# Layer 1's attention scores: a pair's half products issued in two steps, and later blocks' moves queued behind the fourth pair's copies

## The chip, the cores and the metric

The kernel runs on one core of one Trainium2 chip. The metric is the device time of one execution in microseconds (us); before the change three runs had a median of 2338.59 us. In the profile PE is TensorE (matrix products; PEld its weight loads), DVE is VectorE, ACT is ScalarE, POOL is GpSimd and SP is SyncE, which here only issues DMAs. "L753" is line 753 of the kernel before; the change moves later lines by a few (L753 becomes L756, L835 becomes L839, L852 becomes L856).

## The reference

The reference computes two layers in float32. Layer 0 is a convolution-style attention with 8 heads on 8 batch elements of 1024 positions and 256 channels. Layer 1 is what the change touches, followed by a mixture of 8 experts:

```python
def _L1_attn_ref(x, W):
    xa = jnp.einsum('bnd,ed->bne', x, W)
    scores = jnp.einsum('bne,bme->bnm', xa, x)
    attn = jax.nn.softmax(scores, axis=-1)
    return jnp.einsum('bnm,bmd->bnd', attn, x)

x = _L0_conv_ref(x, ...)
t = _to_tokens(x)
t = t + _L1_attn_ref(_ln_t(t), L1_attn_W)
t = t + _L1_ffn_ref(_ln_t(t), router_w, w1, b1, w2, b2)
```

So for each batch element there is a 1024 x 1024 matrix of scores, a softmax over its rows, and a product of the result with the 1024 x 256 normalised tokens.

## The kernel before

The eight batch elements are worked on one after the other. An element goes through layer 0 (`layer0`), then layer 1's attention (`attend`), then a norm and the router. Elements 0 to 6 are sent to the experts sorted by expert, all together near the end (`experts`); element 7 goes through all experts densely (`dense`), while the sorted results of the others are gathered and added beside it.

In `attend` the 1024 rows of scores are eight blocks of 128 rows. The scores are made by Strassen's scheme in the form with seven products: the sums and differences of the operands are `s1_` to `s4_` and `t1_` to `t4_`, and two blocks, k and k+4, form a `Pair`. A pair needs seven half products of 128 x 512 results (L753). They go to three places in PSUM: `x` and `v` are the two halves of one tile of 1024 columns (`both`, the profile's `ps`), and `z` is a tile of its own (`ps1z`). The products into `x` accumulate, and between them the intermediate sum is copied out by ACT: the first copy (L741) after a11 b11, the second (L745) after s2 t2 is added, the third (L748) after s3 t3 is added. Each of the next products into `x` therefore waits for the copy before it. DVE then adds `v` or `z` to a copy and takes the row minimum in the same instruction (`add`, L763). `rest` adds the last two products, ends the row maxima (L763 and L791), and ACT takes the exponentials (L786, L795, L803).

A block of exponentials must be transposed before the mixing, which is the product with the tokens. `turn` does it without TensorE: DVE transposes squares of 32 x 32 (L824), and sixteen moves (L835) bring the squares to their places, eight as ACT copies and eight as DMAs that SP issues, in turns. `turn_now` does it on TensorE for the first and the last block (L842, `pa`). `mix` is the mixing: eight products of 128 x 256 into `py` (L852), then DVE adds the result to the tokens (L861). The mixings run in the order of the blocks 0, 4, 1, 5, 2, 6, 3, 7; the profile's numbers for `py` in this text are block numbers. The code's own names `first`, `second`, ... `eighth` follow that same order.

The order of the instructions on each engine is made by the program before it runs: the statements are recorded, and a list scheduler with its own costs sets them in order under their data dependencies. `tc.issue_after(a)` asks that what follows stand behind `a`; `tc.declare_no_dep` takes a dependency away. Each engine then runs its list strictly in order. Elements 1 to 6 have the same order as one another. Elements 0 to 6 also have parts of the next element's layer 0 between the mixings (`pv`, L408). In element 7 DVE also adds the gathered expert results (`o`, L1400), placed by the table `PLACES` behind named steps of the attention.

Of the kernel before, what the change touches and what calls it, by code (L numbers as in the profile page):

```python
# [12 lines left out]
AF = mybir.ActivationFunctionType  # L13
# [6 lines left out]
def kernel(  # L20
# [23 lines left out]
    nc = tc.nc  # L44
    P = 128
# [43 lines left out]
    def big(name):  # L89

        return ps_big.tile([P, 1024], F32, tag="big", name=name)

    def acc(name):

        return ps_acc.tile([P, 512], F32, tag="acc", name=name)
# [234 lines left out]
    evicted = {}  # L330
# [342 lines left out]
    def attend(b, t1, fill, tick=nothing):  # L673
# [13 lines left out]
        HALF = S // 2  # L687
# [3 lines left out]
        t1_, t2_, t3_, t4_ = (mixes[:, i, :] for i in range(4))  # L691
# [5 lines left out]
        s1_, s2_, s4_ = (mixes[:, 4 + i, :] for i in range(3))  # L697
# [27 lines left out]
        class Pair:  # L725

            def __init__(self, k):
                self.k = k
                both = big(f"ps1_{b}_{k}")
                self.x, v = both[:, :HALF], both[:, HALF:]  # L730
                self.z = acc(f"ps1z_{b}_{k}")
                self.ex = [homes[EX[2 * k + h]] for h in range(2)]
                self.low = [
                    small.tile([P, 1], F32, tag=f"nlow{h}", name=f"nlow_{b}_{k}_{h}")
                    for h in range(2)
                ]
                left, right = (self.ex[0][:, ts(n, HALF)] for n in range(2))
                far = self.ex[1][:, ts(1, HALF)]
                at = ts(k, P)
                self.product(self.x, a11, b11, True)  # L740
                self.first = nc.scalar.copy(left, self.x)  # L741
                second = self.product(v, a12, b21, True)
                tc.declare_no_dep(second.ins, self.first.ins, reason="the other bank")
                self.product(self.x, s2_, t2_, False)
                self.second = nc.scalar.copy(right, self.x)  # L745
                self.product(self.z, s1_, t1_, True)
                self.product(self.x, s3_, t3_, False)
                nc.scalar.copy(far, self.x)  # L748
                self.add(left, v, 3.0e38, self.low[0])
                self.add(far, self.z, 3.0e38, self.low[1])  # L750

            def product(self, to, stationary, moving, start):
                return nc.tensor.matmul(  # L753
                    to,
                    stationary[:, ts(self.k, P)],
                    moving,  # L756
                    start=start,
                    stop=True,
                    skip_group_check=not start,
                )  # L760
# [10 lines left out]
                    accum_out=to,  # L771
                )

            def rest(self):
                k = self.k
                self.product(self.z, s4_, b22, False)
                self.product(self.x, a22, t4_, False)
                nmax, ssum = [], []
                for h in range(2):
                    nmax.append(small.tile([P, 1], F32, tag="nmax", name=f"nmax_{b}_{2 * k + h}"))  # L780
                    ssum.append(small.tile([P, 2], F32, tag="ssum", name=f"ssum_{b}_{2 * k + h}"))
                ex0, ex1 = self.ex

                def even():
                    tick(("max", 2 * k), self.add(ex0[:, HALF:], self.z, self.low[0], nmax[0]))
                    nc.scalar.activation(  # L786
                        ex0, ex0, AF.Exp, bias=nmax[0], scale=-1.0, accum_out=ssum[0][:, 0:1]
                    )

                def odd():  # L790
                    last = nc.vector.tensor_scalar(  # L791
                        scrap, self.x, -1.0, self.low[1], ALU.mult, ALU.min, accum_out=nmax[1]
                    )
                    tick(("max", 2 * k + 1), last)
                    nc.scalar.activation(  # L795
                        ex1[:, :HALF],
                        self.x,
                        AF.Exp,
                        bias=nmax[1],
                        scale=1.0,  # L800
                        accum_out=ssum[1][:, 0:1],
                    )
                    nc.scalar.activation(  # L803
                        ex1[:, HALF:],
                        ex1[:, HALF:],
                        AF.Exp,
                        bias=nmax[1],
                        scale=-1.0,
                        accum_out=ssum[1][:, 1:2],
                    )  # L810

                for half in (odd, even) if k == 1 else (even, odd):
                    half()
                return [(2 * k, ex0, ssum[0][:, 0:1], None), (2 * k + 1, ex1, *self.halves(ssum[1]))]
# [4 lines left out]
        def turn(i, ex, behind=None):  # L819


            at_sq, at_aT = SQ_AT[i]
            sq = homes[at_sq]
            nc.vector.transpose(sq, ex)  # L824
            if at_aT is None:
                aT = two.tile([P, S], F32, tag="tr", name=f"aT_{b}_{i}")
            else:
                aT = homes[at_aT]
            to = aT.rearrange("p (m a q) -> p a m q", a=NQ, q=SQ)
            since = sq.rearrange("p (m k q) -> p k m q", k=NQ, q=SQ)  # L830
            for a in range(NQ):
                for k in range(NQ):
                    move = nc.sync.dma_start if (a + k) % 2 else nc.scalar.copy
                    with tc.issue_after(behind[a * 2 // NQ].ins) if behind else nullcontext():
                        move(to[ts(k, SQ), a], since[ts(a, SQ), k])  # L835
            return [aT[:, ts(m, P)] for m in range(NT)]
# [10 lines left out]
        def mix(at, aT, ssum, more):  # L847
            i = BLOCKS[at]
            ahead = fill("last products") if at == NT - 1 else None
            py = acc(f"py_{b}_{i}")  # L850
            for m in range(NT):
                evicted["mixed"] = nc.tensor.matmul(  # L852
                    py[:, :D], aT[m], n1[:, m, :], start=(m == 0), stop=(m == NT - 1)
                )
            rs = small.tile([P, 1], F32, tag="rs1", name=f"rs1_{b}_{i}")
            if more is not None:  # L856
                nc.vector.tensor_add(rs, ssum, more)
                ssum = rs
            nc.vector.reciprocal(rs, ssum)
            with tc.issue_after(ahead.ins) if ahead else nullcontext():  # L860
                mixed = nc.vector.scalar_tensor_tensor(  # L861
                    t2[:, i, :], py[:, :D], rs, t1[:, i, :], ALU.mult, ALU.add
                )
            tick(("mixed", at), mixed)
# [3 lines left out]
        def turned(at, ex, ssum, more, behind=None):  # L868
            return at, turn(at, ex, behind), ssum, more

        pairs = [Pair(0), Pair(1)]
        first, second = pairs[0].rest()
        second = turned(*second)
        third, fourth = pairs[1].rest()
        now = turn_now(0, first[1])
        pairs.append(Pair(2))
        third = turned(*third, (pairs[2].first, pairs[2].second))
        fourth = turned(*fourth, (pairs[2].second, pairs[2].second))
        mix(0, now, *first[2:])
        mix(*second)  # L880
        fifth, sixth = pairs[2].rest()
        fifth = turned(*fifth)
        mix(*third)
        pairs.append(Pair(3))
        sixth = turned(*sixth, (pairs[3].second, pairs[3].second))
        mix(*fourth)
        seventh, eighth = pairs[3].rest()
        seventh = turned(*seventh)
# [3 lines left out]
        now = turn_now(7, eighth[1])  # L892
# [428 lines left out]
    class Results:  # L1321
# [96 lines left out]
        def tick(self, place, behind=None):  # L1418
            added, sent, stored = self.PLACES.get(place, (0, 0, 0))
            if place == ("max", 0):  # L1420
                self.scored = behind
            if added:
                with tc.issue_after(behind.ins):
                    for _ in range(added):
                        self.add()
            for _ in range(sent):
                self.gather(behind)
            for _ in range(stored):
                if self.whole:
                    b, total, n = self.whole.pop(0)  # L1430
                    store(b, total, n)
# [135 lines left out]
    for b in range(B):  # L1567
# [18 lines left out]
        def fill(place):  # L1586

            nonlocal norm
            others.tick(place)
            if place == "last products":  # L1590
                norm = Norm(t1, one.tile([P, NT, D], F32, tag="xa", name=f"n2_{b}"), 1e-5, f"f{b}")
                return norm.blocks(0, NT - 1)
# [46 lines left out]
```

## Time and profile before

| what | value |
|---|---|
| three runs | 2336.98, 2345.87, 2338.59 us |
| median | 2338.59 us |
| the profiled execution's own time | 2327.18 us |
| its span | 2325.2 us |
| mean granted TensorE clock | 0.993 |
| PE busy | 2259.1 us, 97% of the span |
| DVE, ACT, POOL busy | 67%, 50%, 18% |
| `attend`, px to the last py, elements 1 to 6 | 67.03 to 67.53 us each |
| the same of element 0 | 74.76 us |
| the same of element 7 | 73.15 us |

Times are microseconds from the span's start. A row of the timeline gives the start, the length of a merged run of instructions, the engine, the line, the operation and the tiles, the count, and in brackets the idle time of the engine just before it with what ended that idle time. A half product is recorded as two passes of TensorE ("x2"). PE rows overlap a little, since a product's end is recorded after the next has begun.

### The profile page before, as it was taken

To read this page: it belongs to the slowest core of one execution; us is meant where nothing else is said; L and a number is where in the kernel's file an instruction comes from. 1 tells how busy PE (TensorE), PEld (TensorE's weight loads), DVE (VectorE), ACT (ScalarE), POOL (GpSimd) and SP (SyncE) were. 2 spreads that over 40 slices of the span, in tenths; PEclk is the share of its full clock that TensorE was granted. 3 is DMA by queue.
4 is the path that set the end of the run, shared out by engine and by line. 5 is a ranking of instruction groups with operands and counts; after the bars stand their busy time and mean duration, and the time that the engine had idled before them with its cause. 6 is when DMAs were issued, how large, how long until landed. Compare 5 with 4: busy or idle time off the path is not lost.

```text
span 2325.2 us, 37960 instructions
## 1 busy us (share of the span) xinstructions
PE 2259.1 (97%) x13059; PEld 1211.7 (52%) x13059; DVE 1561.8 (67%) x4029; ACT 1167.0 (50%) x2139; POOL 411.2 (18%) x392
## 2 busy tenths in 40 slices
PE   9999999999999999999999999999999899999798
PEld 3344634563356335643554355435553278886565
DVE  5775678567865786578757775677668756435765
ACT  3664466356635663656464656465546532224311
POOL 0000012000200030003000200021002124544663
PEclk9999999999999999999999999999999999999899
DMA  8995201020102010201020101100120237765664
GB/s 293 385 386 156 69 12 45 4 61 8 49 1 55 12 53 1 46 19 51 6 40 25 44 13 24 41 21 17 19 45 19 71 90 196 194 190 156 189 201 134
DMA packets 278759, 200.10 MB, mean 86 GB/s; under 512 B 189576, under 2 KB 232232, under 8 KB 276776
## 3 DMA queue, kind: packets, MB, share of 16 engines
q1 hardware_dynamic: 252472, 139.14, 21.3%
q0 software_dynamic: 25008, 58.01, 7.8%
q8 instruction: 104, 1.70, 0.3%
q10 hardware_dynamic: 1088, 0.52, 0.1%
q14 instruction: 87, 0.71, 0.1%
HBM read 108.88 MB, written 110.90 MB: 95 GB/s over the span
## 4 chain that ended last, share of the span: by engine, by line
PE 80%; ACT 6%; DVE 5%; DMA 4%; issue 3%; SPq 1%; POOL 0%; DVEq 0%; ACTq 0%; POOLq 0%
PE po L569 19%; PE psc L492 18%; PE pqk L371 7%; PE py L852 6%; PE pr L666 5%; PE pv L408 4%; PE ps L753 3%; PE ph L1256 3%; PE pe L1282 3%; PE pdy L1529 2%; PE pdh L1505 2%; PE px L703 2%; PE pqk L349 2%; DMA y<-yb 1%; ACT aT L835 1%
## 5 line engine op out<-in xcount | busy, mean ns | idle before, releaser
L533 ACT ACTIVATE ex<-psc,nmax 128x1024 f32<-128x1024 f32 x512 | 570.5, 1115 | 309.9 <-DVE scrap L516 225.9
L569 PE MATMUL po<-ex,vs 64*64 64x512 f32 x4096 | 569.6, 593 | 10.7 <-SPq L579 9.8
L492 PE MATMUL psc<-qk,qk 64*64 64x512 f32 x4096 | 573.0, 593 | 3.6 <-ACT ex L533 3.5
L516 DVE TENSOR_SCALAR_CACHE_REDUCE scrap<-psc,nmax 128x512 f32<-128x512 f32 x512 | 384.4, 751 | 166.6 <-PE psc L492 138.7
L507 DVE TENSOR_REDUCE nmax<-psc 128x1 f32<-128x512 f32 x512 | 350.3, 684 | 9.3 <-PE psc L492 9.3
L492 PEld LDWEIGHTS psc<-qk,qk 64*64 64x64 f32 x4096 | 178.7, 132 | 281.1 <-ACT ex L533 131.5
L569 PEld LDWEIGHTS po<-ex,vs 64*64 64x64 f32 x4096 | 173.1, 132 | 287.8 <-issue 84.2
L1070 POOL DMA_INDIRECT rows<-n,d_at x112 | 109.0, 973 | 663.6 <-DVE nmax L507 663.3
L997 POOL TENSOR_TENSOR t<-t,n 128x2048 f32<-128x2048 f32 x8 | 36.3, 4536 | 876.8 <-DVE n L263 876.8
L371 PE MATMUL pqk<-xT,wqkv 128*128 128x512 f32 x384 | 171.2, 599 | 0.0
L336 ACT ACTIVATE qk<-pqk,b_qks 128x512 f32<-128x512 f32 x124 | 85.6, 690 | 86.6 <-PE pqk L371 77.5
L371 PEld LDWEIGHTS pqk<-xT,wqkv 128*128 128x128 f32 x384 | 71.0, 190 | 99.9 <-issue 76.5
L1378 POOL DMA_INDIRECT yk<-y,yat x112 | 111.4, 995 | 60.4 <-issue 25.6
L408 PE MATMUL pv<-wqkv,xT 128*128 128x512 f32 x256 | 120.3, 599 | 1.6 <-DVE v L416 1.0
L852 PE MATMUL py<-n,spare 128*128 128x256 f32 x512 | 118.0, 386 | 3.9 <-DMA out_dram<-oT 3.2
L852 PEld LDWEIGHTS py<-n,spare 128*128 128x128 f32 x512 | 98.3, 193 | 29.0 <-issue 16.4
L666 PE MATMUL pr<-wo,res 128*128 128x256 f32 x512 | 111.9, 379 | 0.0
L835 ACT COPY spare<-home 32x256 f32<-32x256 f32 x256 | 103.0, 402 | 10.1 <-DVE home L824 6.7
L666 PEld LDWEIGHTS pr<-wo,res 128*128 128x128 f32 x512 | 97.2, 190 | 17.0 <-ACT res L588 3.2
L1266 ACT ACTIVATE hb<-ph,wb 128x256 f32<-128x256 f32 x96 | 40.4, 471 | 125.4 <-issue 84.0
L533 ACT ACTIVATION_READ_ACCUMULATOR ex<-psc,nmax 128x1 f32 x512 | 99.1, 194 | 0.0
L1256 PE MATMUL ph<-xb,wb 128*128 128x256 f32 x384 | 91.8, 381 | 5.7 <-DMA wb<-wpack,w_at 4.1
(256 smaller groups left out, 2889.6 us busy)
## 6 DMA issues: line engine op xcount, KB each, us to landing
rows<-wb SPq DMA_DIRECT2D x7, 8192.0 KB
xr<-rows SPq DMA_DIRECT2D x252, 64.0 KB
y<-yb POOLq DMA_DIRECT2D x63, 256.0 KB, 2.6
xs<-in_x_dram SPq DMA_DIRECT2D x64, 128.0 KB
spare<-home SPq DMA_DIRECT2D x256, 32.0 KB
out_dram<-oT SPq DMA_DIRECT2D x60, 128.0 KB
xT<-in_x_dram SPq DMA_DIRECT2D x7, 1024.0 KB
sums<-t SPq DMA_DIRECT2D x7, 1024.0 KB
```

The source lines that it names most:

```text
L371: mm = nc.tensor.matmul(pq[:, ts(n, 512)], wqkv[:, cc, t, ts(g, P)], xT[:, cc, ts(n, 512)], start=(cc == 0), stop=(cc == NCC - 1),)
L408: nc.tensor.matmul(pv, self.xT[:, cc, ts(i, P)], wqkv[:, cc, 2, :], start=(cc == 0), stop=(cc == NCC - 1),)
L492: mm = nc.tensor.matmul(pss[at, h][ts(c, DK), ts(n, 512)], k[r, j * P + c * DK : j * P + (c + 1) * DK], q[r, ts(n, 512)], start=True, stop ...
L507: firsts[at, h] = nc.vector.tensor_reduce(nmax, pss[at, h][:, ts(0, 512)], AX.X, ALU.max, negate=True)
L516: seconds[h] = nc.vector.tensor_scalar(scrap, pss[at, h][:, ts(1, 512)], -1.0, nmaxes[at, h], ALU.mult, ALU.min, accum_out=nmax,)
L533: nc.scalar.activation(ex, pss.pop((at, h)), AF.Exp, bias=nmaxes.pop((at, h)), scale=1.0, accum_out=sums[at][:, h : h + 1],)
L569: mm = nc.tensor.matmul(po[n][ts(h, DK), :], vss[at][keys, h, :], exps[at, h][keys, ts(n, 512)], start=(j == 0 and turn == 0), stop=(j == ...
L666: nc.tensor.matmul(pr[:, :C], res[:, g, ts(i, P)], wo[:, g, :], start=(g == 0), stop=(g == NPAIR - 1))
L835: move(to[ts(k, SQ), a], since[ts(a, SQ), k])
L852: evicted["mixed"] = nc.tensor.matmul(py[:, :D], aT[m], n1[:, m, :], start=(m == 0), stop=(m == NT - 1))
L1256: last = nc.tensor.matmul(ph[:, ts(fc, BR)], wb[:, dc * FF + fc * P : dc * FF + (fc + 1) * P], xb[:, dc, :], start=(dc == 0), stop=(dc == ...
L1378: ins = nc.gpsimd.indirect_dma_start(out=self.slot(at)[:, k, :], out_offset=None, in_=self.group.y[:, :], in_offset=bass.IndirectOffsetOnAxis(
```

## The change

`Pair` no longer issues its first five products in one go. Its constructor issues three of them (a11 b11, a12 b21, s1 t1), the first copy, and DVE's `add(left, v)`. A new step `middle` issues s2 t2, the second copy, s3 t3, the third copy and `add(far, z)`. For pair 2 `middle` stands behind the first mixing. For the pairs before and after it is called where the text shows. The moves of the fifth and sixth block now stand behind the fourth pair's second and third copies. `rest` takes an argument that sets the first block's exponential behind the second pair's third copy. The first mixing is emitted before the turns of the third and fourth block.

```diff
-                left, right = (self.ex[0][:, ts(n, HALF)] for n in range(2))
-                far = self.ex[1][:, ts(1, HALF)]
-                at = ts(k, P)
+                self.left = self.ex[0][:, :HALF]
                 self.product(self.x, a11, b11, True)
-                self.first = nc.scalar.copy(left, self.x)
+                self.first = nc.scalar.copy(self.left, self.x)
                 second = self.product(v, a12, b21, True)
                 tc.declare_no_dep(second.ins, self.first.ins, reason="the other bank")
-                self.product(self.x, s2_, t2_, False)
-                self.second = nc.scalar.copy(right, self.x)
                 self.product(self.z, s1_, t1_, True)
+                self.add(self.left, v, 3.0e38, self.low[0])
+
+            def middle(self, behind=None):
+                far = self.ex[1][:, HALF:]
+                with tc.issue_after(behind.ins) if behind else nullcontext():
+                    self.product(self.x, s2_, t2_, False)
+                self.second = nc.scalar.copy(self.ex[0][:, HALF:], self.x)
                 self.product(self.x, s3_, t3_, False)
-                nc.scalar.copy(far, self.x)
-                self.add(left, v, 3.0e38, self.low[0])
+                self.third = nc.scalar.copy(far, self.x)
                 self.add(far, self.z, 3.0e38, self.low[1])
+                return self
...
-            def rest(self):
+            def rest(self, behind=None):
...
-                    nc.scalar.activation(
-                        ex0, ex0, AF.Exp, bias=nmax[0], scale=-1.0, accum_out=ssum[0][:, 0:1]
-                    )
+                    with tc.issue_after(behind.ins) if behind else nullcontext():
+                        nc.scalar.activation(
+                            ex0, ex0, AF.Exp, bias=nmax[0], scale=-1.0, accum_out=ssum[0][:, 0:1]
+                        )
...
-        pairs = [Pair(0), Pair(1)]
-        first, second = pairs[0].rest()
+        pairs = [Pair(0).middle(), Pair(1).middle()]
+        first, second = pairs[0].rest(pairs[1].third)
         second = turned(*second)
         third, fourth = pairs[1].rest()
         now = turn_now(0, first[1])
         pairs.append(Pair(2))
+        mix(0, now, *first[2:])
+        pairs[2].middle(evicted["mixed"])
         third = turned(*third, (pairs[2].first, pairs[2].second))
         fourth = turned(*fourth, (pairs[2].second, pairs[2].second))
-        mix(0, now, *first[2:])
         mix(*second)
         fifth, sixth = pairs[2].rest()
-        fifth = turned(*fifth)
+        pairs.append(Pair(3))
         mix(*third)
-        pairs.append(Pair(3))
-        sixth = turned(*sixth, (pairs[3].second, pairs[3].second))
+        pairs[3].middle()
+        fifth = turned(*fifth, (pairs[3].second, pairs[3].second))
+        sixth = turned(*sixth, (pairs[3].third, pairs[3].third))
         mix(*fourth)
```

`evicted["mixed"]` is the last product of the latest mixing, and `turned(..., behind)` sets both the ACT half and the SP half of a block's moves behind the two instructions given.

## The prediction

> **What bounds the kernel now.** I read the page's engine rows and its chain first, then a table of the eight stretches of `attend`, then the timelines of PE and ACT inside three of them.
>
> ```profile
> span 2325.2 us, 37960 instructions
> PE 2259.1 (97%) x13059; PEld 1211.7 (52%) x13059; DVE 1561.8 (67%) x4029; ACT 1167.0 (50%) x2139; POOL 411.2 (18%) x392
> PE 80%; ACT 6%; DVE 5%; DMA 4%; issue 3%; SPq 1%; POOL 0%; DVEq 0%; ACTq 0%; POOLq 0%
> ```
>
> PE is the bound nearly everywhere, and the change adds and removes no product. It can only move PE's idle time, of which the whole span has 66 us (2325.2 less 2259.1). The stretches from the first px product to the last mixing (columns: length, then PE, PEld, DVE, ACT and POOL busy, and the granted clock), for elements 1, 0 and 7:
>
> ```profile
> 437.38:504.43 67.05, 64.97 (x226) 40.71 (x225) 36.02 (x85) 40.69 (x89) 0.00 (x0) 1.00 0.24 40
> 189.51:264.27 74.76, 68.93 (x226) 42.26 (x225) 35.99 (x85) 40.62 (x89) 0.00 (x0) 0.95 0.47 104
> 2113.22:2186.37 73.15, 65.39 (x216) 40.41 (x216) 53.22 (x121) 40.68 (x89) 46.69 (x48) 0.95 0.70 188
> ```
>
> PE is idle for 2.08 us in element 1 (2 to 6 are alike), 5.8 in element 0 and 7.8 in element 7. The PE timeline shows where; element 1 first, then element 0:
>
> ```profile
> 464.91 1.12 PE L753 MATMUL ps<-mixes 128*128 128x512 f32 x2 [0.47 <-ACT home L741]
> 467.18 1.12 PE L753 MATMUL ps<-mixes,xa 128*128 128x512 f32 x2 [0.28 <-ACT home L745]
> 481.69 1.12 PE L753 MATMUL ps<-mixes,xa 128*128 128x512 f32 x2 [1.33 <-ACT home L745]
> ...
> 226.39 1.12 PE L753 MATMUL ps<-mixes 128*128 128x512 f32 x2 [2.09 <-ACT home L741]
> 229.50 2.08 PE L753 MATMUL ps<-mixes,xa 128*128 128x512 f32 x2 [1.98 <-ACT home L745]
> 231.36 5.65 PE L852 MATMUL py<-n,aT 128*128 128x256 f32 x16
> ```
>
> Each wait is a product into `x` waiting for ACT's copy of what `x` held. A wait costs 0.26 us more than its bracket: products start 0.86 us apart but are recorded 1.02 long, which hides 0.16, and the product after a wait takes 1.12 instead of 1.02. So element 1 loses 2.08 + 3 x 0.26 = 2.9 us. In element 0 a mixing then takes 5.65 us where the others take 3.62, and a product 2.08 where others after a wait take 1.12. The table by 3.4 us shows why:
>
> ```profile
> 225.23:228.64 3.41, 1.12 (x2) 0.30 (x2) 0.69 (x3) 3.34 (x8) 0.00 (x0) 1.00 0.32 49
> 228.64:232.05 3.41, 2.55 (x4) 1.43 (x5) 0.32 (x2) 1.25 (x4) 0.00 (x0) 0.50 0.06 10
> 232.05:235.47 3.42, 3.42 (x9) 2.70 (x9) 0.70 (x2) 0.14 (x1) 0.00 (x0) 0.50 0.02 5
> ```
>
> After a slice with PE busy for 1.12 us the clock was halved for two slices. Price: 5.65 - 3.62 + 2.08 - 1.12 = 3.0 us. Last, ACT in element 1, on which the moves and the copies queue:
>
> ```profile
> 477.71 3.31 ACT L835 COPY home<-home 32x256 f32<-32x256 f32 x8
> 481.05 0.59 ACT L745 COPY home<-ps 128x512 f32<-128x512 f32 x1
> 481.66 1.65 ACT L835 COPY spare<-home 32x256 f32<-32x256 f32 x4
> 483.33 0.59 ACT L748 COPY home<-ps 128x512 f32<-128x512 f32 x1
> 483.94 1.64 ACT L835 COPY spare<-home 32x256 f32<-32x256 f32 x4
> 487.96 1.15 ACT L786 ACTIVATE home<-home,nmax 128x1024 f32<-128x1024 f32 x1 [2.37 <-DVE nmax L763]
> ```
>
> **The change part by part.** The order of instructions that the changed program holds, set against the old one, is the same outside `attend` on every engine, and the same on SP but for one place in element 7: a load of sums, which waits for a DVE add, now stands ahead of twelve moves. It holds them up by some 2 us (a wait of 1.4 and its issue), which the mixings of blocks 1 and 5, 5 us or more behind their last moves, cover; uncovered it would cost those 2 us. I took the durations of the rows above and walked the new order through one middle element, in the old trace's times.
>
> *First two waits (pair 2).* Old: 0.47 + 0.28 + 2 x 0.26 = 1.27 us. New: s2 t2 stands behind all eight mixing products and one `pv` product, so PE has a free slot at 461.69 (first mixing) + 8 x 0.43 + 0.86 = 466.0. But DVE's `add(left, v)` is now ahead of it in the program, it reads the other half of the tile that s2 t2 writes, and the product waits for it (the program's waits name DVE there; before it was ACT's copy). DVE ends a transposition at 465.67, or 0.15 later because the first pairs' adds are reordered, and the add takes 0.69: 466.45. Idle 0.45, and 0.10 for the restart. Then s3 t3 has its slot at 466.55 + 0.96 + 0.86 = 468.3, but the second copy now has four moves (4 x 0.415) and the fourth pair's first copy (0.59) before it on ACT: 465.85 + 1.66 + 2 x 0.59 = 468.7. Idle 0.45, restart 0.10. Sum 1.1 us: a gain of 0.2 that a late DVE add takes back, so I put it at nil (bounds -0.3 and +0.5 us).
>
> *Third wait (pair 3).* Old 1.33 + 0.26 = 1.59: the second copy stood behind eight moves (the row at 477.71). New: the fifth block's ACT moves stand behind that copy, and s2 t2 behind mixing 1. Its result is there 1.02 us after its start, the copy takes 0.59, so s3 t3 can start at 1.66 and has a slot at 0.86: idle 0.8, restart 0.1, or 0.9. Gain 0.65.
>
> *What ACT pushes back.* s2 t2 now starts at 475.03 + 0.86 + 3.45 = 479.35, so its copy ends at 481.0. Behind it ACT has sixteen moves (6.64) and the third copy (0.59), and only then the seventh block's exponential: 488.2 at the earliest, against 487.96, and 488.6 if ACT waits for the third product. The 2.37 us that ACT had idle before that row was the cover, and ACT spends it idle after 477.7 instead. From this exponential hang a DVE transposition, eight moves on SP at 0.65 us each, and mixing 3. In the trace its last move is issued at 495.09 and, by the semaphore records, lands at 497.05; mixing 3 starts at 497.3 without a wait. With PE 0.65 earlier (496.7) and the moves 0.25 to 0.65 later (497.5), PE waits 0.8 us, and a restart behind a DMA costs up to 0.26. This is a new wait of about 1.05.
>
> Sum for a middle element: 0 - 0.65 + 1.05 = +0.4 us; the bounds are -0.65 (no new wait) and +1.0 (one more ACT move and one SP issue in that chain). Times six: **+2.4 us** (-3.9 to +6).
>
> *Element 0.* Old: 5.8 idle + 6 x 0.26 = 7.3 us. New, walked the same way: 0.5 and 0.6 for pair 2; 0.9 for a22 t4 behind the third copy; 1.7 for pair 3's s3 t3, whose copy stands behind seven moves (2.9 us) that its product outruns by 1.2; 1.3 for the last block's transposes, whose exponential waits in ACT's queue; five restarts at 0.1. Together 5.5, so -1.8 (bounds -2.5, -1.0). The two waits of 2 us are no longer in one slice, so the halved clock should go: -3.0, or 0 if a slice falls badly around the 1.7.
>
> The Trainium skill, in "TensorE: Matmul & The Clock Gate" (section "Why this matters for your kernels"), asks for no PE gap over about 3 us, one idle window returning the clock to half. No gap here was over 2.1 us and the clock halved all the same, so the measurement decides; by the page's rule alone nothing would be owed to the clock in element 0, and the sum would be 3.0 higher.
>
> *Element 7.* Here DVE also adds gathered results, eight to fourteen `o` adds of 0.4 us at a step. In the new order pair 3's `add(left, v)` stands behind some thirteen of them, a store's transposition (1.2) and two maxima, and reaches 2153.7; s2 t2 now waits for that add, where in the trace it started at 2150.59 without a wait. That is 3.1 us of new idle; pair 2's two waits grow by 1.3, and one for the third copy adds 0.9. The old waits of 0.84 and 1.18 go with their 0.5, and so does most of the 1.09 at block 4's mixing. Sum +5.3 - 3.4 = **+1.9** (bounds +0.5, +4). One 3.1 us gap may halve the clock (0 to +3.4, half of 6.8); later waits hide most of it; I take +0.5.
>
> Total: 2.4 - 1.8 - 3.0 + 1.9 + 0.5 = 0.0 us. On the profiled execution's own 2327.18 that is 2327.2; that execution lies 11.4 below the median of the three runs, so on their scale the forecast is 2338.6.
>
> **The rivals.**
>
> *Faster: ACT's queue does not hold the seventh exponential.* If it starts as soon as its maximum is known, mixing 3 does not wait: 6 x -0.65 - 4.8 + 1.9 = -6.8, or 2332 us. For it: ACT is only 61% busy in element 1. Against: the sixteen moves now begin 3.3 us later.
>
> *Slower: ACT's moves late at every mixing.* If each middle element pays +1.0, element 0 keeps its half clock and element 7's gap brings one (+3.4): 6 - 1.8 + 1.9 + 3.4 = +9.5, or 2348 us. The place is ACT between the fourth pair's second copy and the seventh exponential; it decides once that stretch is over 0.65 us longer than the row's start at 487.96 allows. To pass 0.5% (11.7 us) the middle elements would need +1.4 each.
>
> *The change doesn't do what it says.* SP's half of the moves keeps its place, and the freed third product only trades one wait for another: every part near nil but the clock, -3.0 or 0, 2336 to 2339 us. This is hard to tell from the forecast.
>
> **How the numbers follow.** Forecast 0.70 (with the third rival inside it), faster rival 0.12, slower rival 0.18. The range runs from the faster rival's 2332 to the slower one's 2348, which also holds a scatter of medians, the three runs lying 9 us apart. About 0.5% is what a measurement of this kernel can tell from no change; all cases but the far ends lie inside. Slower by more than that 0.08 (the slower rival's tail), faster 0.04 (it would take -2.0 in every element, more than two thirds of the 2.9 that is lost there), the rest 0.88.
>
> **What would show it.** In elements 1 to 6: the first wait named as DVE `nlow`, the third at about 0.6 to 0.8, a new wait at block 3's mixing on `spare` moves, the stretch 67.0 to 68 long. In element 0: no halved clock, about 70 us. In element 7: one idle of 3 us at `ps<-mixes`. I am wrong if a middle element's length moves by over 1 us, or if element 0 keeps its waits of 2 us.

## The result, and the profile after

| | median | lowest to highest | runs |
|---|---|---|---|
| before | 2340.25 us | 2336.98 to 2346.86 | 15 |
| after | 2337.94 us | 2334.14 to 2342.53 | 15 |

The ratio of after to before is 0.9985, 95% interval 0.9976 to 0.9994: 3.5 us less, between 1.4 and 5.6. The forecast of no change, 0.0 us, lies outside that interval; the measured time lies inside the forecast's range. That 2337.94 is so close to the 2338.6 of the forecast is luck: with fifteen runs the kernel before has a median of 2340.25, where three had 2338.59. The profiled execution of the changed kernel took 2334.83 us. The top of its page:

```profile
span 2332.8 us, 37999 instructions
PE 2261.0 (97%) x13059; PEld 1211.5 (52%) x13059; DVE 1558.5 (67%) x4029; ACT 1167.8 (50%) x2139; POOL 411.6 (18%) x392
```

This one execution is longer than the profiled one of before (2325.2), although the median is shorter: single executions say little here, and the comparison has to be made by stretches. The profile of before (2327.18 us) also lies below all fifteen runs of before in this table. Up to the first px product of element 7 that makes no difference: it starts at 2109.22 us here, and at 2108.60 and 2110.35 in two later profiles of the same kernel. From there to the end this execution took 223.57 us and the later ones 214.43 and 212.75, so the rows of element 7 shown here are those of an unusually long execution. The stretches of `attend` for elements 1, 0 and 7 (length, then PE, PEld, DVE, ACT and POOL busy, and the clock):

```profile
432.60:499.97 67.37, 65.37 (x226) 40.53 (x225) 35.74 (x85) 40.54 (x89) 0.00 (x0) 1.00 0.24 40
189.80:259.31 69.51, 65.85 (x226) 40.36 (x225) 35.68 (x85) 40.52 (x89) 0.00 (x0) 1.00 0.51 113
2109.22:2187.95 78.73, 67.82 (x216) 41.40 (x216) 51.26 (x118) 40.84 (x89) 47.34 (x48) 0.93 0.62 167
```

Element 1 is 0.3 us longer than before, element 0 is 5.25 shorter with the clock at 1.00 instead of 0.95, element 7 is 5.6 longer. PE's timeline in element 1:

```profile
461.79 1.13 PE L756 MATMUL ps<-mixes 128*128 128x512 f32 x2 [0.22 <-DVE nlow L766]
464.11 1.13 PE L756 MATMUL ps<-mixes,xa 128*128 128x512 f32 x2 [0.33 <-ACT home L749]
476.31 1.13 PE L756 MATMUL ps<-mixes,xa 128*128 128x512 f32 x2 [0.73 <-ACT home L749]
492.82 3.48 PE L856 MATMUL py<-n,spare 128*128 128x256 f32 x15 [0.72 <-DVE t L865]
```

All four waits stand where the prediction put them. The first is now named as DVE's add (`nlow`), the third has fallen from 1.33 to 0.73, and the fourth is new, at block 3's mixing. (The DVE `t` that is named there ends at 492.62, but it is not what is waited for: in an experiment below the same mixing starts before that DVE instruction does. By the semaphore records the last of block 3's moves lands at 492.58, 0.24 us ahead of the mixing.) ACT in the same element:

```profile
475.67 0.59 ACT L749 COPY home<-ps 128x512 f32<-128x512 f32 x1 [2.67 <-PE ps L756]
...
477.84 0.59 ACT L751 COPY home<-ps 128x512 f32<-128x512 f32 x1
...
480.13 3.31 ACT L839 COPY spare<-home 32x256 f32<-32x256 f32 x8
483.47 1.15 ACT L790 ACTIVATE home<-home,nmax 128x1024 f32<-128x1024 f32 x1
```

The 2.67 us that ACT waits idle before the second copy stand in place of the 2.37 that it was idle ahead of the seventh exponential before. That exponential now starts straight behind the sixteenth move, with no bracket: ACT's queue holds it. Element 0, PE's timeline and the 3.4 us slice that holds its longest wait:

```profile
223.89 1.13 PE L756 MATMUL ps<-mixes,xa 128*128 128x512 f32 x2 [0.58 <-ACT home L751]
227.45 1.12 PE L756 MATMUL ps<-mixes,xa 128*128 128x512 f32 x2 [1.57 <-ACT home L749]
228.41 3.62 PE L856 MATMUL py<-n,aT 128*128 128x256 f32 x16
```

```profile
225.24:228.66 3.42, 1.85 (x6) 0.71 (x5) 1.43 (x4) 3.31 (x8) 0.00 (x0) 1.00 0.30 48
```

PE is busy for 1.85 us in that slice instead of 1.12, and the mixing behind it takes 3.62 us where it took 5.65: the clock is not halved. Element 7:

```profile
2138.53 1.12 PE L756 MATMUL ps<-mixes 128*128 128x512 f32 x2 [1.07 <-DVE nlow L766]
2149.80 1.64 PE L756 MATMUL ps<-mixes 128*128 128x512 f32 x2 [2.32 <-issue]
2152.07 6.17 PE L856 MATMUL py<-n,spare 128*128 128x256 f32 x16 [0.63 <-DMA spare<-home]
...
2193.56 3.60 PE L281 MATMUL pt_n<-ident,n 128*128 128x128 f32 x14 [5.61 <-DVE n L263]
```

The wait of s2 t2 for DVE's add is there (2.32; in a later profile of the same kernel it is named DVE `nlow`), and in this execution the clock was halved behind it: the mixing at 2152.07 takes 6.17 us.

### The profile page after: what moved, and what is told of

It reads as the page before. It is cut to its first block, busy times and chain, and to the rows that moved or that the text cites. A ratio compares the mean times of both kernels' runs of the same rounds, so it can differ in the third digit from the quotient of the medians.

```text
span 2332.8 us, 37999 instructions
## 1 busy us (share of the span) xinstructions
PE 2261.0 (97%) x13059; PEld 1211.5 (52%) x13059; DVE 1558.5 (67%) x4029; ACT 1167.8 (50%) x2139; POOL 411.6 (18%) x392
## 4 chain that ended last, share of the span: by engine, by line
PE 78%; DVE 5%; ACT 5%; issue 5%; DMA 3%; POOL 3%; SPq 1%; another core or an unknown queue 0%; DVEq 0%; ACTq 0%; POOLq 0%
PE po L569 18%; PE psc L492 18%; PE py L856 7%; PE pqk L371 7%; PE pr L666 5%; PE ps L756 4%; PE pv L408 4%; PE ph L1262 3%; PE pe L1288 3%; PE px L703 2%; POOL yk L1384 2%; PE pqk L349 2%; PE ps1z L756 2%; DMA y<-yb 1%; ACT aT L839 1%
## 5 line engine op out<-in xcount | busy, mean ns | idle before, releaser
L516 DVE TENSOR_SCALAR_CACHE_REDUCE scrap<-psc,nmax 128x512 f32<-128x512 f32 x512 | 384.2, 750 | 165.9 <-PE psc L492 137.3
L1384 POOL DMA_INDIRECT yk<-y,yat x112 | 111.7, 997 | 73.4 <-issue 29.2
```

The source lines that it names most:

```text
L516: seconds[h] = nc.vector.tensor_scalar(scrap, pss[at, h][:, ts(1, 512)], -1.0, nmaxes[at, h], ALU.mult, ALU.min, accum_out=nmax,)
L1384: ins = nc.gpsimd.indirect_dma_start(out=self.slot(at)[:, k, :], out_offset=None, in_=self.group.y[:, :], in_offset=bass.IndirectOffsetOnAxis(
```

## The experiments

Twelve kernels ran in three series of four, most of them eleven times and two of them five times. Each was compared with runs of the kernel before in the same series; "saved" and "lost" below are the ratio's distance from 1 times 2328, with its 95% interval. In these three series the kernel before had medians of 2327.91, 2327.49 and 2328.29, some 12 us less than in the series of the result.

### First series: the parts by themselves

The kernel before again, unchanged:

> The kernel before, unchanged, timed against itself and profiled once more. Theory A (the terms of the forecast were right, and the profiled execution of before was typical): ratio 1.000; element 7's attention again near 73 us and from its first px product to the end of the span near 212 us. Theory B (the profiled execution of before had a lucky element 7, and most executions lose some 10 us more there): ratio 1.000, but element 7's attention 75 to 79 us, or from its first px product to the end 218 to 224 us; elements 0 and 1 at 74.8 and 67.05 us as before.

Measured: ratio 1.0002 (0.9992 to 1.0012). Its profile repeats the stretches of before: element 0 74.71, element 1 67.08, element 7 73.28, the halved clock at 228.6. From px of element 7 to the end it took 213.73 us, against 211.94 in the profiled execution of before. So in this series the first profile is a typical one. For the series of the result, which was some 12 us slower, there is no profile of the kernel before.

The next three kernels hold both forms of `attend` and take the new one where a condition on the element holds:

```diff
     def attend(b, t1, fill, tick=nothing):
...
+        if b == 0:          # e0_only; mid_only: 0 < b < B - 1; e7_only: b == B - 1
+            ...             # Pair, rest, turn, mix and the order of the change
         ...                 # the same of before
```

> The new order in element 0 alone, the old one in elements 1 to 7. Theories A and B: element 0's attention near 69.5 us instead of 74.8, no halved clock in it, the time lower by 4.8 to 5.3 us (ratio 0.998). A third theory (the halved clock of element 0 falls only in some executions of before): lower by 2 to 3 us only, ratio 0.999.

Measured: ratio 0.9991 (0.9982 to 1.0), 2.1 us saved. Element 0 took 69.43, no halved clock stands in it, and px of element 1 comes 242.71 us after px of element 0, against 247.83: 5.1 us in the trace. That is more than the runs allow (0.0 to 4.2); where the rest went was not found.

> The new order in elements 1 to 6 alone. Theories A and B: each of them 67.3 to 67.6 us instead of 67.05, the time up by 2 to 2.5 us (ratio 1.001). A fourth theory (the middle elements gain in most executions): down by 2 us or more.

Measured: ratio 1.0010 (1.0001 to 1.0019), 2.3 us lost. Elements 1 to 5 took 67.31, 67.27, 67.56, 67.53 and 67.30, each 0.23 to 0.29 more than in the kernel before of this series; from px of element 1 to px of element 6 it is 1201.88 against 1200.68. The theory that the middle elements gain is out.

> The new order in element 7 alone. Theory A (the forecast's term): up by 2.4 us, or as the profile after has it by 5 or more, ratio 1.001 to 1.002. Theory B: nil or down by up to 2 us, ratio 0.999 to 1.000, since the new 3 us wait only takes the place of waits for late transfers that most executions have.

Measured: ratio 1.0009 (1.0 to 1.0018), 2.1 us lost. Element 7's attention took 77.63, which is 4.35 more, but from its px to the end it is 215.44 against 213.73, only 1.7 more. In this pair of profiles more than half of the loss is given back behind the attention.

The results also list every run's mean granted clock. The 33 runs of before average 0.9918, the 11 runs with only element 0 new 0.9929. That is 2.6 us of full clock in 2328, close to the 3.4 that one halved stretch of 6.83 us takes. In the profiles the halved clock stands in element 0 in all four kernels that have its old form unchanged (from 226.7 or 228.6 us on), and in none of the nine with the new one. So it is there in most executions, not in some.

### Second series: the whole, pairs of parts, and the term of ACT's queue

> The changed kernel itself again, in one series with kernels that hold parts of it. Theory A (the parts add up: element 0 -2.1, elements 1 to 6 +2.3, element 7 +2.1, each measured against before in the first series): +2.3 us against before, element 0 at 69.5, a middle element at 67.3 to 67.6, element 7 at 77 to 79. Theory S (the whole gains 3.5 us, and the parts do not add up, because what element 7 loses is given back when the elements before it are new as well): -3.5 us here too. Theory M (both are within what a series can shift, since the length of the first layer's expert stretch and of the tail differ by several us from one execution to the next whatever the order): between -3 and +2, with the stretches of element 0, of the middle ones and of element 7 as in the parts.

Measured: ratio 1.0 (0.9991 to 1.0009). Element 0 69.42, elements 1 to 5 67.27 to 67.52, element 7 76.62.

> The new order in elements 0 to 6, the old one in element 7. Theory A: +0.2 us against before (-2.1 + 2.3), and 2.1 less than the whole. Theory S: slower than the whole, since the new element 7 belongs to the gain; -1 or more. Theory M: 2 us less than the whole, element 7 at 73 to 74.

Measured: ratio 0.9990 (0.9981 to 0.9999), 2.3 us saved. Element 7 took 73.36. The two kernels differ in element 7 alone, and their rows show how the loss there is given back. DVE's last `o` add before the last norm, and PE's first transposition behind that norm, in the kernel with the old element 7:

```profile
2183.93 0.53 DVE L1579 SCALAR_TENSOR_TENSOR o<-yk,gate,o 128x256 f32<-128x256 f32 x1 [1.69 <-DMA yk<-y,yat]
```

```profile
2187.31 3.48 PE L281 MATMUL pt_n<-ident,n 128*128 128x128 f32 x14 [5.27 <-DVE n L263]
```

and the same in the whole change:

```profile
2185.35 0.44 DVE L1406 SCALAR_TENSOR_TENSOR o<-yk,gate,o 128x256 f32<-128x256 f32 x1
```

```profile
2188.84 3.48 PE L281 MATMUL pt_n<-ident,n 128*128 128x128 f32 x14 [3.62 <-DVE n L263]
```

With the old element 7 DVE waits 1.69 us for a gathered result of the experts before it can normalise; with the new one the result has landed by then. The attention ends 3.3 us later, the transposition starts 1.6 later.

> The new order in elements 0 and 7, the old one between. Theory A: 0.0 us against before (-2.1 + 2.1), and 2.3 less than the whole. Theory S, if the middle elements carry the gain: about +0, that is 3.5 more than the whole. Middle elements at 67.05, element 0 at 69.5 without a halved clock, element 7 at 77 to 78.

Measured: ratio 1.0002 (0.9992 to 1.0012). Elements 1 to 5 67.04 to 67.32, element 6 67.82, element 0 69.43, element 7 74.79. The three kernels of this series lie within each other's intervals, so they do not by themselves decide between the theories; the stretches do.

The fifth block's moves, in the kernel with the old element 7:

```diff
-        fifth = turned(*fifth, (pairs[3].second, pairs[3].second))
+        fifth = turned(*fifth, (pairs[3].first if b else pairs[3].second, pairs[3].second))
```

> As the new order in elements 0 to 6 with the old one in element 7, but in elements 1 to 6 the first half of the fifth block's ACT moves stands ahead of the second copy of pair 3, the second half ahead of its third copy; nothing else in any queue moves. By the forecast's term of what ACT pushes back (+1.05 a middle element: twelve moves in place of sixteen stand between the second copy and the seventh exponential, so that it starts 1.66 us earlier) the wait at block 3's mixing, 0.72 in the changed kernel, goes to 0 to 0.1, the third wait stays at 0.7, and a middle element falls by 0.7 to some 66.8: 4.3 us less than the kernel with the new order in elements 0 to 6, about -4 against before. The rival (the exponential is not held by ACT's queue but by its maximum, or block 3's moves by SP): the wait stays at 0.7 and the middle elements at 67.4, no difference. A third way: the four moves hold up the second copy, the third wait grows by as much as the other shrinks, and the length stays.

Measured: ratio 0.9964 (0.9950 to 0.9977), 8.4 us saved, with five runs. The third wait stays, the new one is gone (PE, and then ACT's seventh exponential, in element 1):

```profile
475.81 1.12 PE L757 MATMUL ps<-mixes,xa 128*128 128x512 f32 x2 [0.68 <-ACT home L750]
...
487.99 7.11 PE L857 MATMUL py<-n,spare 128*128 128x256 f32 x32
```

```profile
482.08 1.15 ACT L791 ACTIVATE home<-home,nmax 128x1024 f32<-128x1024 f32 x1 [0.71 <-DVE nmax L767]
```

The two mixings of blocks 6 and 3 now merge into one run of 32 products without a gap. ACT waits for the maximum again, so its queue holds the exponential no more. The edit also frees four of SP's moves, but SP is not what held block 3 up: counted from px, it issues the moves of the fifth and sixth block at the same times with the edit and without it (within 0.03 us). Without it SP then stands idle from 51.3 to 53.4 us behind px, until DVE's transposition of the seventh block has ended at 53.3. With it that transposition ends at 52.4, and SP goes on at 52.5. Elements 1 to 5 took 66.35 to 66.60, each 0.9 less than with the whole change; from px of element 1 to px of element 6 it is 1197.52 against 1202.19 in the kernel without this edit: 4.7 us for five elements. The term of what ACT pushes back is shown, at 0.9 an element for the forecast's 1.05.

### Third series: the clock by itself, the wait in element 7, and one step further

Before, with four products repeated in element 0:

```diff
+                if b == 0 and k == 3:
+                    self.again(v, (self.first,), pairs[2].fourth)
-                self.product(self.x, s2_, t2_, False)
+                third = self.product(self.x, s2_, t2_, False)
                 self.second = nc.scalar.copy(right, self.x)
+                if b == 0 and k == 3:
+                    self.again(v, (self.first, self.second), third)
...
+            def again(self, v, copied, behind):
+                for _ in range(2):
+                    with tc.issue_after(behind.ins):
+                        more = self.product(v, a12, b21, True)
+                    for copy in copied:
+                        tc.declare_no_dep(more.ins, copy.ins, reason="the other bank")
```

> The kernel before, with four products repeated in element 0: a12 b21 of pair 3 is computed again twice behind s4 b22 of pair 2 (into the two waits of 2 us that PE has there) and twice behind its s2 t2; each is 0.86 us, the results are the same, no other queue changes. It parts the clock from the waits. By the forecast's clock term (-3.0, because a slice in which PE was busy 1.13 us halves the clock for 6.83 us) the slice at 225.2 now has PE busy over 2.5 us, the halved clock at 228.6 goes, element 0 falls from 74.7 to 71.3 while the waits for ACT's copies stay where they were, and the median falls by 3.0 to 3.4 us, if a gain in element 0 reaches the end. If it doesn't (element 0 new alone measured -2.1, where its stretch was 5.1 shorter), element 0 falls by 3.4 and the median by 1 or so. If the halving has another cause than PE's idle slice, nothing changes, or it is up to 0.5 slower for products that overrun the waits.

Measured: ratio 0.9991 (0.9982 to 1.0), 2.1 us saved. The products fill the waits, and the copies come when they came before (PE in element 0, and the slice):

```profile
224.11 1.88 PE L764 MATMUL ps<-nT,xa 128*128 128x512 f32 x4
226.36 1.13 PE L764 MATMUL ps<-mixes 128*128 128x512 f32 x2 [0.38 <-ACT home L741]
...
229.47 1.13 PE L764 MATMUL ps<-mixes,xa 128*128 128x512 f32 x2 [0.26 <-ACT home L747]
```

```profile
225.23:228.64 3.41, 3.03 (x8) 1.06 (x6) 0.67 (x3) 3.33 (x8) 0.00 (x0) 1.00 0.31 49
```

s2 t2 and s3 t3 start at 226.36 and 229.47, where they started at 226.39 and 229.50 before. Only the clock differs: no halved stretch stands in element 0, whose length is 71.82 instead of 74.71. The clock's term is 2.9 us, for the forecast's 3.0. Work that nobody needs, put into a wait, makes the kernel's first element faster.

The whole change with the dependency on DVE's add taken away in element 7 (the products read and write the bank of `x`, the add reads the bank of `v`):

```diff
-                self.add(self.left, v, 3.0e38, self.low[0])
+                self.added = self.add(self.left, v, 3.0e38, self.low[0])
...
-                    self.product(self.x, s2_, t2_, False)
+                    fourth = self.product(self.x, s2_, t2_, False)
+                if b == B - 1:
+                    tc.declare_no_dep(fourth.ins, self.added.ins, reason="the other bank")
...
-                self.product(self.x, s3_, t3_, False)
+                fifth = self.product(self.x, s3_, t3_, False)
+                if b == B - 1:
+                    tc.declare_no_dep(fifth.ins, self.added.ins, reason="the other bank")
```

> The changed kernel, but in element 7 the products s2 t2 and s3 t3 are declared independent of DVE's add of the left half, which reads the other bank of the same tile; the order of instructions is the same on every engine, only these waits change. By the forecast's element 7 (3.1 us of idle because s2 t2 waits for that add; 2.33 in the trace) the idle at block 5's place goes to 0.5 or less and element 7's attention falls by 2 us or so, from 76.6 to 74.5. What reaches the end by the theory that the next wait on DVE's normalisation swallows half (5.27 us of it with the old element 7, 3.62 with the new one): 1.0 to 1.3 us less than the whole in this series. Rival: the add's wait only stood ahead of one for ACT's copy, and the idle stays near 2 us; then no difference.

Measured: ratio 1.0008 (0.9999 to 1.0017). My expectation was wrong; the rival is right in that nothing is gained, though the idle moved on instead of staying. Element 7's waits:

```profile
2142.43 1.13 PE L760 MATMUL ps<-mixes,xa 128*128 128x512 f32 x2 [1.89 <-ACT home L751]
2151.75 3.69 PE L860 MATMUL py<-n,spare 128*128 128x256 f32 x16 [1.31 <-DMA spare<-home]
2157.61 1.12 PE L760 MATMUL ps<-mixes,xa 128*128 128x512 f32 x2 [1.31 <-ACT home L755]
```

s2 t2 no longer waits at all in either pair, but the next steps wait longer by about as much: 1.89 for a copy of pair 2 (1.05 and 0.68 at its two products in the whole), 1.31 for block 1's moves (0.62 in the whole). Element 7 took 75.38, where the whole took 76.62 and 75.73 in two executions. PE's idle in that attention is 11.26 us, against 11.12 and 10.01. DVE's add was only the first of several things that were late there.

The last one goes a step further than the fifth block's earlier moves, again with the old element 7; in elements 1 to 6 only:

```diff
+            def third_product(self, behind=None):
+                with tc.issue_after(behind.ins) if behind else nullcontext():
+                    self.product(self.x, s2_, t2_, False)
+                self.second = nc.scalar.copy(self.ex[0][:, HALF:], self.x)
...
         pairs.append(Pair(3))
+        if 0 < b < B - 1:
+            pairs[3].third_product()
         mix(*third)
-        pairs[3].middle()
-        fifth = turned(*fifth, (pairs[3].second, pairs[3].second))
+        pairs[3].middle()   # without s2 t2 and its copy where they went ahead
+        fifth = turned(*fifth, (pairs[3].second, pairs[3].second) if not 0 < b < B - 1 else None)
```

> As the kernel with the fifth block's moves earlier, but in elements 1 to 6 pair 3's s2 t2 stands ahead of block 1's mixing instead of behind it, its copy ahead of all of the fifth block's ACT moves, and the third copy behind those eight moves. s3 t3 then has mixing 1 (3.45 us) between it and s2 t2: the third wait, 0.73 us in a middle element, goes to nil, the second copy is done under the mixing. Ahead of the seventh exponential stand the eight moves of the sixth block and the third copy as before. The middle elements fall from 66.4 to 65.7, or 4 us for the six. Rival: s2 t2 waits for DVE's add of the left half (named as DVE nlow), which comes later than PE there; then a wait of 0.5 or so takes the place of the 0.73, and the gain is 1 us or less.

Measured: ratio 0.9958 (0.9944 to 0.9971), 9.8 us saved, with five runs: the lowest ratio of all. PE in element 1:

```profile
470.62 1.02 PE L761 MATMUL ps<-mixes 128*128 128x512 f32 x2
471.47 3.62 PE L861 MATMUL py<-n,spare 128*128 128x256 f32 x16
474.93 1.02 PE L761 MATMUL ps<-mixes,xa 128*128 128x512 f32 x2
```

A whole mixing lies between s2 t2 and s3 t3, and neither waits. From px of element 1 to px of element 6 it took 1193.70, another 3.8 less than with the fifth block's moves earlier; 0.7 for each element was expected. Between the two kernels' medians (2321.16 and 2317.30, in different series) that difference is not told apart from scatter.

> The changed kernel in a third series, since two series gave -3.5 and 0.0 us against before, each within 2. By the stretches of the traces (element 0 -5.2, elements 1 to 6 together +1.2 to +1.7, px of element 7 to the end +1.6) it is -2.0 in all. If this series lies between -3.5 and 0.0, that sum stands and each of the two was a scatter to one side; if it is -3.5 again, something gains that the stretches do not show; if 0.0 or above, the first layer's expert stretch or the tail takes back some of element 0's gain.

Measured: ratio 0.9996 (0.9984 to 1.0009), 0.9 us saved, between 3.7 saved and 2.1 lost. It lies between the two series before. Weighted by their intervals, the three series of the whole change (-3.5, 0.0 and -0.9) give -1.6 us, with 1.3 to each side.

## Why the prediction was wrong where it was

The forecast was a sum of terms that cancelled exactly: 0.0, where the result is 3.5 us less. Their places were right, and three sizes were off to the same side. All lengths here are against the kernel before of the first series, but for element 7's, which are means.

| stretch | forecast | by the traces |
|---|---|---|
| element 0, px to px of element 1 | -4.8 | -5.1 (242.7 against 247.83) |
| elements 1 to 6 | +2.4 | +1.5 for five of them (1202.18 against 1200.68) |
| element 7, px to the first transposition behind the last norm | +2.4 | +1.5 |
| sum | 0.0 | -2.1 |

The row of element 7 sets the four profiles of the three series that hold the change there (78.20 to 81.25 us, mean 79.73; the kernel without the dependency left out) against the eight with the old element, the profile of before among them (77.20 to 80.21, mean 78.27). From px to the end of the kernel the two means are 213.7 and 213.1, only 0.6 apart, and the sum would be -3.0. But behind that transposition all these kernels have the same order, and the rest still took 133.5 to 137.3 us, so the further 0.9 is taken as scatter. The profile of the result's own series is left out of the four: its 84.3 and 223.6 us would by themselves raise the two differences to +2.4 and +2.6, as much as the forecast. Element 6 is left out of the middle row, because its lengths scatter, from 67.0 to 67.8 in the old order and from 67.2 to 68.1 in the new.

*Element 7 is the step that failed most by these traces.* The term was +1.9 of waits in the attention and +0.5 of clock. The waits in the attention cost more than that: 74.8 to 77.6 us in the same four profiles, mean 76.2, against 73.2 to 74.3 in the eight, mean 73.4, so +2.8. But I carried the term to the end of the kernel as if nothing lay in between. Before the last norm DVE waits for a gathered result of the experts (the row with 1.69 us above), and that hides part of the lateness. With the old element one of DVE's last two `o` adds there has this wait in six of the eight profiles (0.67 to 3.31 us), with the new one in none. In the pair of kernels that differ in element 7 alone half of the loss is gone at the first transposition (3.3 to 1.6 us). The medians are too coarse to tell: with the new element 7 alone they lose 2.1 us, between 0.0 and 4.2, which has room for the forecast too. Inside the attention, s2 t2 waits 2.3 us for the forecast's 3.1. The moves of block 1, which the prediction called covered, are not always so: its mixing waits 0.62 us for them in the whole.

*The middle elements.* Pair 2's two waits: forecast nil; block 4's mixing starts 32.45 us behind px instead of 32.48, so nil. The third wait: forecast -0.65; measured -0.6 (s3 t3's bracket 1.33 to 0.73). The new wait at block 3's mixing: forecast 0.8 and a restart of 0.26, together 1.05; measured 0.67 in the brackets and 0.16 beside it in the second series, 0.83 in all. This size, of what ACT pushes back, was too large by 0.2 in each element. The sum is +0.2 to +0.3 instead of +0.4. The faster rival, in which ACT's queue does not hold the seventh exponential, is out: that row has no bracket, and moving four of the sixteen ACT moves ahead of the second copy took the wait away. The slower rival put all ACT moves late at every mixing and is out too; only block 3's is late.

*Element 0.* The change does here what it says. The halved clock: forecast -3.0; -2.9 when it alone was removed. The idle: forecast -1.8; 5.83 to 3.58 us in the gaps, -2.2. The longest wait left is 1.57 us at s3 t3 of pair 3, forecast 1.7.

Two slips in the working change nothing: 5.8 and 6 x 0.26 make 7.4 and not 7.3 for the old element 0, and pair 2's second wait comes out of its own two times at 0.3 and not 0.45 (measured 0.33).

*What stays open.* The sum of the stretches, -2.1 or -3.0, lies within the interval of the result's -3.5 (1.4 to 5.6 less). Of the three series together, -1.6 with 1.3 to each side, -2.1 lies inside and -3.0 just outside; against the 0.0 of the second series, with 2.1 to each side, -2.1 lies at the edge and -3.0 outside. That all of element 0's 5.1 reaches the end is not shown either: with element 0 alone the runs save 2.1. The stretch from px of element 6 to px of element 7, which holds element 6's attention, element 7's layer 0 and the experts, took 474.1 to 478.4 us in fourteen profiles, without a pattern by the kernel, and the halved clocks behind it vary likewise. This is large enough to move one series of medians by 3 us, but that it did so was not shown.

## What to carry to other kernels

A wait that is shortened on the bound engine by holding back work on another engine is paid for where that work is next needed: here moves held behind two copies cost 0.83 us in every middle element, more than the 0.6 that the shortened wait had gained, and putting four of them ahead of the second copy saved it. Where terms of both signs cancel, each needs its own stretch and its own experiment, and a loss near the end is carried to the last instruction through every wait that lies between. The length of each of elements 1 to 5 mostly repeats to 0.1 us from profile to profile where whole runs scatter by 5, so changes of 1 us are read from stretches and not from medians.

## What the runs showed of the hardware

The granted clock follows how much work PE had in a slice of 3.41 us. In element 0, with 1.12 us of work the clock was halved for 6.83 us; with 1.85 (after) and 3.03 (products repeated) it stayed at 1.00, and with the repeated products every wait for a copy ended at the same time as before. Laid on the grid that the starts of the halved stretches form, the slices at full clock of all fourteen profiles (the first 20 us and the last 3 left out) agree: behind less than 1.41 us of PE work the next slice was at half clock all 66 times, behind 1.41 to 1.9 us 8 times of 34, and behind more never but for the slices of the next paragraph. (In the changed kernel's profile of the third series 1.81 us at 1836.54 was followed by half clock; 1.85 in element 0 was not.)

Busy time is not the whole of it. One kind of slice was followed by half clock although PE was busy throughout, here in the kernel before:

```profile
2217.34 3.90 PE L1493 MATMUL pb<-b_rows,gT 8*128 8x256 f32 x16
```

```profile
2218.61:2222.03 3.42, 3.42 (x16) 2.40 (x15) 2.64 (x4) 0.00 (x0) 2.57 (x3) 1.00 1.01 332
2222.03:2225.44 3.41, 3.41 (x10) 2.67 (x9) 0.88 (x2) 0.00 (x0) 1.25 (x2) 0.50 0.39 126
```

These sixteen products have operands of only 8 rows. They fill 2.62 us of the first slice. In eleven profiles they fill 2.19 to 3.26 us of a slice and the next one is at half clock; in the other three they fill at most 2.10 and it is not. This fits products of 8 rows counting for little or nothing, but no experiment here parts it from other causes.

The Trainium skill, in "TensorE: Matmul & The Clock Gate" (section "Why this matters for your kernels"), speaks of a single gap of about 3 us; here two neighbouring waits of 2.09 and 1.98 us, of which one slice held most, were enough. A gap of the size that the page names also cost clock: behind the wait of 3.44 us at 2174.33 in element 7 (after) the mixing took 5.29 us.

The halved stretches late in the kernel are not the same from run to run. Around 2190 us one profile of the changed kernel shows 3.4 us at half clock twice with a full slice between them, another of the same kernel 13.7 us in a row. That need not cost anything where PE waits anyway: from the first transposition behind the last norm to the end the first took 134.2 us and the second 133.5.
